# Layer 0's product of the attention with h by seven products on halves, in a two-layer graph kernel

## The chip, the cores and the metric

The kernel runs on one core of one Trainium2 chip. Its measure is the device time of one execution in microseconds, from start to end. An engine's name in the profile is short: PE is the tensor engine (PEld its loading of weights), DVE the vector engine, ACT the scalar engine, POOL the GpSimd engine, SP the queue that issues most transfers. All numbers are float32, and every result of PE goes to PSUM, which the program divides into banks of 512 float32 per partition.

## The reference

Sixteen graphs (B) of 1024 nodes (N) with 128 features (D) go through two layers. What matters here, with the names of the reference:

```python
h = jnp.einsum('bnf,df->bnd', x, Ww) + Wb                      # layer 0
e = jnp.einsum('bjl,bkl->bjk', jnp.einsum('bjd,dl->bjl', h, A), h)
e = e + jnp.swapaxes(e, 1, 2)
scores = jnp.where(adj > 0, e, 0.0)
attention = jax.nn.softmax(scores, axis=1) * adj
h_prime = jax.nn.relu(jnp.einsum('bij,bjk->bik', attention, h))
ic = jax.nn.sigmoid(h_prime @ wi_u + x @ wi_x)[..., None]      # fc, oc in the same way
x = _layernorm(x + oc * jnp.tanh(ic * h_prime + fc * x))

h = jnp.einsum('bnf,hfd->hbnd', x, conv_w) + conv_b            # layer 1, four heads
scores = jnp.einsum('hbni,hij,hbmj->hbnm', h, attn_w, h)
Ah = jnp.tanh(adj * scores)
hh = jax.nn.relu(jnp.einsum('hbnm,hbmd->hbnd', Ah, h))
x = _layernorm(x + jax.nn.relu(jax.nn.relu(jnp.mean(hh, axis=0)) + x))
```

The change concerns the one line `attention` times `h` of layer 0: a product of 1024 x 1024 by 1024 x 128 for each graph.

## The kernel before

**Passes and slots.** After a fill, the kernel makes 16 passes, one for each graph b (the loop at L1163). A pass has 32 steps: four heads of layer 1 by eight blocks of 128 rows. In each step PE makes two scores of layer 1 (`Pair.score`, L820, 512 columns each) and, between them, products of earlier steps (`early`, L905, and `late`, L913). Layer 1's product of tanh with h is already done by seven products on halves: `Pair.product` (L845) issues instructions of 64 output columns with 256 columns streamed, two side by side, and `differ` (L838), `differ_more` (L889) and `join_rows` (L788) make the sums and differences that it needs. `differ_more` does one addition on DVE and one by a DMA that accumulates, issued from POOL (L892). `mm` (L80) splits any other product into two instructions of 64 output columns with up to 512 streamed.

Each step has two *slots*, 64 in a pass. Everything else is a small piece with a name, and the lists `PLAN`, `FIRST` and `LAST` (L1128 to L1157), written out by hand, say in which slot each piece is issued. All engines take their work in the program's order, so the plan fixes every queue. A plain name is a piece of layer 0 of the next graph (b + 1), a name with `+` one of the graph after it (b + 2); `d`, `m`, `j`, `r` and `u` are pieces of layer 1, `e` the end of the last graph's layer 1.

**Layer 0 of one graph, by names.** `W`, `X`, `L` load x transposed, x and the rows of adj (the ring of three buffers, L372). `Q` and `H`, `h` make projections, among them h in `t["h"]` (L399). `S` (L419) makes the score blocks, of which only one triangle is computed, into the tile R of 8 x 8 blocks; `T` turns a block row through DRAM (`hop`, L292: one write, and four reads issued later by `land`). `E` makes a mask from adj on POOL (L475). `A` (L508) masks row j and takes its maximum (DVE, L492), negates that (L500, on DVE but for graph 0) and takes exponentials (ACT, L504). `B` (L512) multiplies row j by adj (DVE, L527) and scales h's row by the reciprocal sum (L524).

**The product in question.** `back(j)` (L531) adds row block j's share to the transposed result: for each half q of the 1024 nodes one `mm` with h's row block as weights and 512 columns of R streamed. For a graph b > 0 there is one PSUM bank, `acc0`, used in two turns: for half 0, `B` of each row calls `back` for the row before it; `R0` (L550) ends it and writes relu into `hpT`; then `G0` to `G7` make half 1 in the same bank, and `R1` ends it. In a middle pass `R0` stands in slot 18 (counted from 0), `G0` to `G7` and `R1` in 19 and 20.

**What follows it.** `P` (L610) turns `hpT` into rows (a transposition on DVE, L329, and a hop). `Y`, `F`, `f`, `i`, `o` make the gates from it: a product with the weights on POOL (L620), a sum on DVE (L626), a sigmoid. `I` (L659) and `O` (L671) make the layer's output, `Va` to `Vd` and `N` its layernorm, `D` turns it for layer 1.

**PSUM.** Three banks with the tag `sc` are shared by layer 1's scores and all projections and layer 0 scores, in turn; `acc1` to `acc3` hold layer 1's sums, `acc0` layer 0's.

## Time and profile before

| | us |
|---|---|
| median of 2 runs | 2328.44 (2328.14 to 2328.74) |
| the profiled execution | 2329.8 |
| its span, first to last instruction | 2328.0 |
| PE busy / PEld busy | 2304.9 / 1074.7 |
| DVE / ACT / POOL busy | 2039.5 / 1292.4 / 1308.2 |
| all DMA engines, share of the span: hardware queue, software queue | 38.8%, 18.1% |
| PE busy in the first 65 us / from 65 to 146 us | 62.76 / 77.09 |
| PE busy in the last 146 us | 138.44 |

One execution was profiled. Busy times say how long at least one instruction of an engine was under way; matmuls overlap, so a busy PE can be less than a full one. A group of the profile's list gives the line, the engine, the operation, what is written and read, the shape and the count, then busy time and mean duration in ns, and after a second bar the engine's idle time before such instructions and what ended it. One matmul instruction leaves two records in the trace[...]; two instructions of 64 columns that lie side by side run at once, so four records belong together. A pass takes 2328 / 16 = 145.5 us on average, the fill included.

### The profile page before, as it was taken

Reading aid. Unit: us, or ns where it says so; the run is one execution under the profiler, and the core shown is the slowest. Engines: PE = TensorE matmul, PEld = TensorE weight load, DVE = VectorE, ACT = ScalarE, POOL = GpSimd, SP = SyncE. Lnnn points to the kernel's source line nnn. Section 1 sums busy time; section 2 is a strip of 40 time slices with the busy share of each in tenths; the row PEclk is TensorE's granted clock in tenths of the full one; section 3 lists DMA queues with packets and bytes.
Section 4 is the critical chain, followed back from the end, with each engine's and each line's share of the span. In section 5 each row is a group of like instructions: output and inputs, shape, how many; then the busy total and the mean of one; then the engine's idle time right before and its main releaser. Section 6 shows DMA issues by size and latency. Waiting matters only on the chain. (4 is left out here: it accounts for less than half of the span.)

```text
span 2328.0 us, 40444 instructions
## 1 busy us (share of the span) xinstructions
PE 2304.9 (99%) x14693; PEld 1074.7 (46%) x14693; DVE 2039.5 (88%) x3689; ACT 1292.4 (56%) x2186; POOL 1308.2 (56%) x1129
## 2 busy tenths in 40 slices
PE   9999999999999999999999999999999999999998
PEld 5345544444444444444444444444444444444444
DVE  7879898998989889898898988889898898988777
ACT  6545564555556555555555555556556555554444
POOL 2645656556565655656466564665645646555342
PEclk9999999999999999999999999999999999999999
DMA  4647565575655656556565565756647565573421
GB/s 146 164 95 199 124 144 154 114 195 133 170 133 111 190 137 173 132 123 173 134 180 129 129 179 114 184 133 135 171 105 201 130 165 135 106 184 86 123 55 37
DMA packets 498090, 327.27 MB, mean 141 GB/s; under 512 B 391139, under 2 KB 416482, under 8 KB 497891
## 3 DMA queue, kind: packets, MB, share of 16 engines
q1 hardware_dynamic: 459149, 250.68, 38.8%
q0 software_dynamic: 38448, 73.94, 18.1%
q8 instruction: 116, 1.90, 0.3%
q14 instruction: 83, 0.68, 0.1%
q10 hardware_dynamic: 294, 0.07, 0.0%
HBM read 199.04 MB, written 59.51 MB: 111 GB/s over the span
## 5 line engine op out<-in xcount | busy, mean ns | idle before, releaser
L86 PE MATMUL sc<-uT,x1T 128*64 128x512 f32 x4096 | 1054.4, 593 | 4.0 <-ACT uT L283 1.9
L836 ACT ACTIVATE pair<-pair 128x1024 f32<-128x1024 f32 x504 | 533.3, 1058 | 588.9 <-DVE pair L829 278.7
L892 POOL DMA_DIRECT2D pair<-pair x252 | 225.5, 895 | 723.3 <-ACT pair L836 158.2
L831 DVE TENSOR_TENSOR pair<-sc,adj 128x512 f32<-128x512 f32 x504 | 339.1, 682 | 105.1 <-PE sc L86 103.7
L86 PEld LDWEIGHTS sc<-uT,x1T 128*64 128x64 f32 x4096 | 294.1, 137 | 293.8 <-issue 156.8
L829 DVE SCALAR_TENSOR_TENSOR pair<-sc,adj 128x512 f32<-128x512 f32 x504 | 343.0, 684 | 86.0 <-PE sc L86 81.5
L475 POOL TENSOR_SCALAR edge<-ring 128x1024 uint8<-128x1024 f32 x120 | 361.0, 3010 | 25.2 <-DMA ring<-in_adjT_dram 23.4
L840 DVE TENSOR_TENSOR pair<-pair 128x1024 f32<-128x1024 f32 x252 | 328.8, 1305 | 10.6 <-ACT pair L836 10.6
L864 PE MATMUL late<-pair,h 128*64 128x256 f32 x2016 | 304.8, 380 | 3.7 <-DMA pair<-pair 3.6
L864 PE MATMUL early<-pair,h 128*64 128x256 f32 x2016 | 304.1, 379 | 1.3 <-ACT pair L836 1.3
L864 PE MATMUL late<-pair,hx 128*64 128x256 f32 x2016 | 304.1, 380 | 0.0
L864 PEld LDWEIGHTS early<-pair,h 128*64 128x64 f32 x2016 | 145.3, 137 | 289.7 <-issue 255.2
L86 PE MATMUL acc<-R,h 128*64 128x512 f32 x960 | 232.2, 592 | 1.3 <-ACT h L524 1.3
L864 PEld LDWEIGHTS late<-pair,h 128*64 128x64 f32 x2016 | 145.6, 137 | 185.4 <-issue 129.5
L864 PEld LDWEIGHTS late<-pair,hx 128*64 128x64 f32 x2016 | 146.6, 137 | 178.3 <-issue 142.7
L891 DVE TENSOR_TENSOR pair<-pair 128x512 f32<-128x512 f32 x252 | 187.8, 745 | 3.2 <-PE early L864 2.6
L504 ACT ACTIVATE R<-R,nmax 128x1024 f32<-128x1024 f32 x126 | 144.7, 1148 | 62.8 <-DVE nmax L500 56.4
L492 DVE CUSTOM_DVE_ANT_0 R<-R,edge 128x1024 f32<-128x1024 f32 x120 | 172.8, 1440 | 3.3 <-POOL edge L475 3.0
L527 DVE TENSOR_TENSOR R<-R,ring 128x1024 f32<-128x1024 f32 x120 | 161.6, 1347 | 0.0
L864 PE MATMUL early<-pair,hx 128*64 128x256 f32 x1008 | 152.0, 379 | 0.0
L620 POOL TENSOR_TENSOR x1T<-hp,wu_b 128x1024 f32<-128x1024 f32 x45 | 111.7, 2482 | 69.5 <-DVE hws L626 63.3
L936 POOL TENSOR_TENSOR w<-w 128x512 f32<-128x512 f32 x63 | 84.8, 1346 | 96.5 <-DVE w L926 96.3
(214 smaller groups left out, 2831.2 us busy)
## 6 DMA issues: line engine op xcount, KB each, us to landing
adj<-in_adjT_dram SPq DMA_DIRECT2D x128, 512.0 KB, 4.2
pair<-pair POOLq DMA_DIRECT2D x252, 256.0 KB, 3.7
ring<-in_adjT_dram SPq DMA_DIRECT2D x120, 512.0 KB, 5.0
xT<-in_xT_dram SPq DMA_DIRECT2D x16, 512.0 KB, 7.2
x<-in_x_dram SPq DMA_DIRECT2D x16, 512.0 KB, 5.2
dram_hp<-turn_hp SPq DMA_DIRECT2D x15, 512.0 KB, 2.6
hp<-dram_hp SPq DMA_DIRECT2D x60, 128.0 KB, 3.1
dram_x<-turn_x SPq DMA_DIRECT2D x15, 512.0 KB
```

The lines of the kernel that those rows point to most:

```text
L86: nc.tensor.matmul(out[ts(c, HD)], lhsT[:, ts(c, HD)], rhs, start=start, stop=stop)
L475: engine.tensor_scalar(m, t["adj", j], 0.0, None, ALU.is_gt)
L492: nc.vector.tensor_tensor_reduce(to[:, ks], s[:, ks], t["edge", j][:, ks], 1.0, nmax, ALU.mult, ALU.max, top)
L504: nc.scalar.activation(row(j), row(j), AF.Exp, bias=t["nmax", j], accum_out=t["z", j])
L527: nc.vector.tensor_mul(s[:, ks], s[:, ks], adj[:, ks])
L829: nc.vector.scalar_tensor_tensor(to, psv, -1.0, adj, op0=ALU.mult, op1=ALU.mult)
L831: nc.vector.tensor_mul(to, psv, adj)
L836: nc.scalar.activation(s, s, AF.Tanh)
L840: nc.vector.tensor_add(t[:, X3 : N12 + 1 : N12 - X3, :], t[:, N12 : N12 + 1, :].to_broadcast([P, 2, 512]), t[:, B22 : B11 + 1, :],)
L864: nc.tensor.matmul(out[ts(q, HD)], w, self.t[:, at, ts(q, HN)], start=(i == 0 and p in (1, 3, 5, 4)), stop=(i == BH - 1), skip_group_check ...
L891: nc.vector.tensor_add(t[:, B22], t[:, B22], t[:, N12])
L892: nc.gpsimd.dma_start(t[:, N21], t[:, B22], accum_op=ALU.add)
```

## The change

For graphs from 1 on (graph 0, done in the fill, keeps its way), the product is made by seven products of halves in place of eight. R is cut into four quarters: `block(i, r)` is row block i or i + 4 and half 0 or 1 of the columns, r = 0 to 3. h is cut by row block (i or i + 4) and by feature half.

- `row_sides` (pieces `K0`, `K1`, `K2`) makes the sums and differences of h's quarters in place and in a new tile `x7`, nine subtractions on POOL.
- `product0` (pieces `a`, `c`, `p`, `q`, `y`, `x`, `z` with i = 0 to 3) issues two instructions of 64 by 256 each, 56 a pass.
- `add_blocks` (pieces `s`, `g`, `t`, `v`) adds quarters of R in place: for i = 3 on DVE, for i = 0 to 2 by an accumulating DMA issued from POOL. Between the products the order is: `c` reads quarter 3, `s` adds quarter 1 to 3, `p` reads 3, `g` adds 0 to 1, `q` reads 1, `t` adds 0 to 3, `x` reads 3, `v` adds 3 to 2, `z` reads 2.
- The bank `acc0` has three turns, begun by `a0`, `p0` and `y0`. `gather` (pieces `U1` to `U6`) brings each turn into `hpT`: U1 and U2 are copies on ACT, U3 to U6 additions and subtractions on DVE. `relu_rows` (`R1`) makes the relu there.
- The result's features stand in another order: Ww's transposed columns, Wb's row and the identity of the gate product are permuted when made, one small product is added to the weights' preparation (`p_gu`), and `P` uses `turn_sums` (eight reads with runs of 256 bytes) for `turn` (four with 128); `sum_hp` and `inner` index accordingly.
- The negation of the maximum (L500) moves to ACT for all graphs from 1 on, and `B` no longer calls `back` for them.
- The plans are written anew; pass 14 has one of its own, `NEXT`.

```diff
-            if b == 0 and j > 2:
+            if b or j > 2:
                 nc.scalar.mul(nmax, top, -1.0)
...
-            if j and (b or j not in (1, NB - 1)):
-                back(j - 1, [0] if b else range(NH))
+            if b == 0 and j not in (0, 1, NB - 1):
+                back(j - 1)
...
+        def block(i, r):
+            j, c = divmod(r, NH)
+            return t["R"][:, ts(c, BH), i + j * BH, :]
+
+        def row_sides(n):
+            if n == 0:
+                t["x7"] = sb.tile([P, BH, HD], F32, tag="x7", name=f"x7_{b}", bufs=1)
+            h = t["h"][:, :, :D].rearrange("p (m i) (e d) -> p m e i d", m=2, e=2)
+            g = (slice(0, 3), slice(3, BH), slice(0, BH))[n]
+            x = t["x7"][:, g]
+            a11, a21, a12 = h[:, 0, 0, g], h[:, 0, 1, g], h[:, 1, 0, g]
+            if n == 2:
+                nc.gpsimd.tensor_sub(x, x, a11)
+                return
+            nc.gpsimd.tensor_sub(a12, a11, a12)
+            nc.gpsimd.tensor_sub(x, a21, h[:, 1, 1, g])
+            nc.gpsimd.tensor_sub(a12, a12, x)
+            nc.gpsimd.tensor_sub(a21, a11, a21)
+
+        def product0(p, i):
+            if i == 0 and p in (2, 7, 1):
+                t["acc"] = ps_acc.tile([P, 512], F32, tag="acc0", name=f"acc0_{b}_{p}")
+            h = t["h"][:, :, :D].rearrange("p k (e d) -> p k e d", e=2)
+            j, e, r, at = {
+                2: (i + BH, 0, 2, 0), 3: (i + BH, 0, 3, 1), 7: (i, 1, 3, 0), 5: (None, 0, 1, 1),
+                1: (i, 0, 0, 0), 6: (None, 0, 3, 0), 4: (i + BH, 1, 2, 1),
+            }[p]
+            w = t["x7"][:, i] if j is None else h[:, j, e]
+            for q in range(NH):
+                nc.tensor.matmul(
+                    t["acc"][ts(q, HD), ts(at, HN)], w, block(i, r)[:, ts(q, 2)],
+                    start=(i == 0 and p in (2, 7, 1)), stop=(i == BH - 1),
+                    skip_group_check=True,
+                )
+
+        def add_blocks(n, i):
+            to, a = ((3, 1), (1, 0), (3, 0), (2, 3))[n]
+            to, a = block(i, to), block(i, a)
+            if i == BH - 1:
+                nc.vector.tensor_add(to, to, a)
+            else:
+                nc.gpsimd.dma_start(to, a, accum_op=ALU.add)
+
+        def gather(n):
...
+            if n == 1:
+                nc.scalar.copy(w[:, 0:2], acc)
+            elif n == 2:
+                nc.scalar.copy(w[:, 2:4], acc[:, 0:1].to_broadcast([P, 2, HN]))
+            elif n == 3:
+                nc.vector.tensor_sub(
+                    w[:, 1:4:2], w[:, 1:4:2], acc[:, 1:2].to_broadcast([P, 2, HN])
+                )
+            elif n == 4:
+                nc.vector.tensor_add(w[:, 0], w[:, 0], acc[:, 0])
+            elif n == 5:
+                nc.vector.tensor_add(
+                    w[:, 1:4], w[:, 1:4], acc[:, 0:1].to_broadcast([P, 3, HN])
+                )
+            else:
+                nc.vector.tensor_add(w[:, 2], w[:, 2], acc[:, 1])
+
+        def relu_rows():
+            w = t["hpT"].rearrange("p (k n) -> p k n", k=4)
+            nc.scalar.activation(w[:, 0:4:2], w[:, 0:4:2], AF.Relu)
+            nc.scalar.activation(w[:, 1:4:2], w[:, 1:4:2], AF.Relu, scale=-1.0)
...
-            turn(t["hp"], hpT, f"hp_{b}")
+            turn_sums(t["hp"], t["hpT"], f"hp_{b}")
...
+    PLAN = [
...
+        "r6 r3 m1 B5 L7", "", "E7 +L0 j0.1 e u1.0 A6", "a0 a1 +W", "B6 A7", "a2 u1.1 K0",
+        "d2 c0 c1 s0 +Q0 s1 m2 c2 B7 d3", "s2 a3 +Q1 K1", "e g0 g1 m3 g2 c3 U1 u2.0",
+        "s3 p0 e p1 j1.0", "e p2 q0 t0 e p3", "q1 g3 e U2 t1 t2", "q2 v0 q3 U3",
+        "y0 y1 t3 y2 v1 d4 y3 K2 U4 v2", "e x0 v3 x1 x2 m4 z0 x3", "z1 z2 z3 U5 U6 j1.1 R1",
+        "P d5 +H0", "m5 +h0", "j2.0 +E0", "+S0 e", "d6 m6", "u2.1", "+T0 Y j2.1", "e +L1 F",
...
+        "+S7 +B1 +L4", "+A2 +E3", "", "r4 u0.0 u0.1 d14 m14 r5 r0 d15 +A3 +B2 +T4 +T5 +L5 +B3 r1",
+    ]
...
-        plan = LAST if b + 1 == B else PLAN if b else FIRST
+        plan = FIRST if b == 0 else LAST if b + 1 == B else NEXT if b + 2 == B else PLAN
```

The parts of `PLAN` shown are slots 9 to 32 and the last four, 60 to 63. Between the pieces of two slots PE makes one score of layer 1 and one or two of its early or late products, so that a name in this list stands a known number of PE instructions behind any other.

## The prediction

> **What bounds the kernel now.** I read the page's totals first, then a table of stretches over middle passes, the tensor engine's timeline there, its waits, and last the groups of instructions and single lines.
>
> ```profile
> span 2328.0 us, 40444 instructions
> ...
> PE 2304.9 (99%) x14693; PEld 1074.7 (46%) x14693; DVE 2039.5 (88%) x3689; ACT 1292.4 (56%) x2186; POOL 1308.2 (56%) x1129
> ...
> PEclk9999999999999999999999999999999999999999
> ```
>
> PE is busy 99% of the span at full clock. A busy PE need not be a full one, so I look inside.
>
> ```profile
> core 0: us, PE busy (x) PEld busy (x) DVE busy (x) ACT busy (x) POOL busy (x), PEclk, DMA share, GB/s
> 582.00:728.00 146.00, 145.80 (x946) 66.66 (x942) 130.72 (x235) 82.18 (x140) 84.26 (x71) 1.00 0.61 147
> 1018.00:1164.00 146.00, 145.80 (x944) 66.63 (x942) 131.95 (x237) 82.26 (x138) 86.07 (x72) 1.00 0.60 146
> ```
>
> A middle pass has 0.2 us without PE work. DVE has about 15 us free in it (146 less 131), ACT 64, POOL 62.
>
> ```profile
> 681.46 5.32 PE L86 MATMUL acc<-R,h 128*64 128x512 f32 x24
> 686.61 1.03 PE L86 MATMUL sc<-uT,x1T 128*64 128x512 f32 x4
> 687.47 0.60 PE L864 MATMUL early<-pair,h 128*64 128x256 f32 x4
> 687.90 1.89 PE L86 MATMUL acc<-R,h 128*64 128x512 f32 x8
> 689.61 1.03 PE L86 MATMUL sc<-uT,x1T 128*64 128x512 f32 x4
> ```
>
> The columns are start, duration and count; durations overlap, so the price is the distance between starts. Four records (two instructions of 64 columns, side by side) of 512 cost 687.47 - 686.61 = 0.86 us; 24 of them 5.15, six times 0.86. Four records of 256 cost 687.90 - 687.47 = 0.43, exactly half: the narrower form loses nothing.
>
> ```profile
> PE late L864 <- DMA pair<-pair: 3.6, 4, 1.2
> PE sc L86 <- DVE h L411: 3.1, 12, 0.8
> ...
> PE acc L86 <- ACT h L524: 1.3, 1, 1.3
> ```
>
> The worst of PE's waits are a few us in the whole run. So the kernel is bound by the number of matrix columns streamed, and every us of stream removed is a us of time, if nothing comes late.
>
> **The change, part by part.**
>
> *Stream removed.* The groups give the count:
>
> ```profile
> L86 PE MATMUL acc<-R,h 128*64 128x512 f32 x960 | 232.2, 592 | 1.3 <-ACT h L524 1.3
> ...
> L892 POOL DMA_DIRECT2D pair<-pair x252 | 225.5, 895 | 723.3 <-ACT pair L836 158.2
> ```
>
> 960 records are 240 groups of four, 16 in each of 15 passes: 240 x 0.86 = 206.4 us. After, a pass has 7 products x 4 row blocks x 2 instructions of 256 = 28 groups at 0.43; 15 x 28 x 0.43 = 180.6. PE's stream falls by 25.8 us, 1.72 a pass. One more 128x3 product in the weights' preparation costs at most 0.3 (the row of a 128x128 product is 278 ns), once.
>
> *DVE, per pass.* Added: four block additions (i = 3) at 0.745 (the 128x512 addition of L891) = 3.0; the gathers 3 to 6: one like L926 (128x512 from PSUM, 0.687), two of 256 columns like L925 (0.42), and one of 768, not in the trace: between 0.687 and two of these, 1.37; by the step from 256 to 512 it is 0.95, taken. Together 2.5. Removed: eight negations at 0.154 = 1.2. Net +4.3, so 131 becomes some 135 in a pass of 143.6. DVE's 15 us of free time hide it; they shrink to about 8.5. Without that cover the 4.3 us would be paid, more than twice the gain.
>
> *ACT.* Two copies of 0.58 (L900's first form) for U1 and U2, eight negations at some 0.2 (L632's 128x16 takes 0.217); the two ReLUs only change shape (0.6 each, L548). +2.8 on 82, hidden by 60 us of idle. Below nothing is possible too: with the negation on ACT an exponential no longer crosses from DVE for it; I take nothing.
>
> *POOL.* Twelve accumulating DMAs to issue at 0.895 = 10.7 and nine subtractions: four of 128x192, four of 128x64, one of 128x256. L797 takes 0.457 for 128 columns and L936 1.275 for 512, about 2.1 ns a column: 4 x 0.59 + 4 x 0.32 + 0.73 = 4.4. Together +15 on 85, of 143.6: 70% busy. The sum has cover; the order matters (below).
>
> *DMA and SP.* L892's transfers are 66 of the software queue's 74 MB, and that queue fills 18.1% of 16 engines' span: 2328 x 0.181 x 66/74 / 252 = 1.5 us of all engines each. Twelve add 18 us a pass to a share of 0.61 (89 us). The hp rows are read back by eight DMAs with runs of 256 bytes, no longer four with 128, so 2048 packets fewer; at the hardware queue's mean (38.8% x 2328 x 16 / 459149 = 31 ns) that gives back 4 us. SP issues four more at 0.68; its queue has about 1100 issues in the run, a third of the span. Hidden. The loads of x, xT and the ring change slots; SP takes its issues in order, so a load that waits for its buffer holds back the hops behind it. That costs nothing while what a hop brings is used slots later (a slot is 145.5 / 64 = 2.3 us on average), and at most the hop's own 2.5 to 3.1 us of landing where it is used at once; taken nothing, as the new plan leaves slots between them.
>
> *Waits added on PE, all in front of layer 1's scores, since PE takes its work in order.* Read off the new order, in PE's own us:
> 1. c0 needs the first three subtractions of K0, which may only start after a2. Between them lie a projection, a score and a late product: 2.58 us. The subtractions take 3 x 0.59 = 1.8, and more when POOL is held up: L796 has a median of 773 ns against L797's 457. Nothing to 1.5; taken 0.1.
> 2. a3 needs row block 7 weighted (L527, mean 1.35) by DVE, which stands behind a score eviction, a 1.3 and a 0.745 addition and a reciprocal. From the score that releases this to a3 PE has 4.3 us of other work; the DVE row sums to 0.68 + 1.3 + 0.75 + 0.16 + 1.35 = 4.2. No slack: nothing to 1.4; taken 0.2.
> 3. One PSUM bank in three turns: p0 waits for U1's copy on ACT, with 2.58 us of PE work in between, while ACT has a 0.58 and a 0.37 copy, a 1.06 tanh and then U1's 0.58 to do. Nothing to 2.6; taken 0.2. y0 waits for U3 on DVE, with 1.7 us for a 0.69 operation behind one eviction; 0.1.
> 4. The pass boundary. Slot 63 now issues rows 2 and 3 of the next layer 0 at once: on DVE a mask (1.44), two weightings, two small turns, two pair additions; on ACT the first tanh of the next pass stands behind the exponentials of row 4 (1.15 and 0.19) and two copies. Adding rows from the end of the pass's last score: exponentials 3 end at 7.3 us (behind the evictions of two projections and r0), the weighting of row 3 at 8.6, an eviction and the mask of row 4 at 10.4, exponentials 4 at 11.9, the copies at 12.9, the tanh at 13.9; PE, with nothing late, wants it at 13.3. Nothing to 0.9; taken 0.3.
> 5. Block additions: see the second rival. Taken nothing.
>
> That is 0.9 a pass, 13.5 us in 15.
>
> *A rule against the change.* L840 adds two operands from SBUF:
>
> ```profile
> L840 DVE TENSOR_TENSOR pair<-pair x252: 1198/1217/2607, 72.6 to 2289.5; 128x1024 f32<-128x1024 f32 x126
> ...
> L797 POOL TENSOR_TENSOR hx<-hx,h x126: 453/457/1411, 62.2 to 2260.4; 128x128 f32<-128x128 f32 x126
> ```
>
> Its mean of 1305 is 107 above its least, with single ones at twice the length. The Trainium skill ("SBUF — State Buffer", section "Who interferes with whom") says that DVE with two SBUF inputs and GpSimd exclude each other on a shared port pair, one waiting for the whole instruction of the other. By the rows, some 45 such DVE operations a pass lose 0.1 each, 4.5 us; POOL's arithmetic grows from 70 to 75 us, so 7% more: 0.3 us. By the rule at its worst all nine new POOL operations (4.4 us) stand in DVE's way, and the four new additions wait half of a 2.9 us mask (L475): +10, DVE over 143 of 143.6 and no slack left. The means hold such collisions already; I take 0.3, within DVE's free time.
>
> **Sum.** The profiled execution took 2329.8 (span 2328.0 and 1.8 around it), 1.4 above the median. 2329.8 - 25.8 + 13.5 = 2317.5; less 1.4: about 2316.
>
> **Rivals.**
> *The gain is eaten by small waits* (2326 to 2340). DVE's margin falls from 15 to 8.5 us; points 1 to 4 come to a third of their upper bounds together: (1.5 + 1.4 + 2.6 + 0.9) / 3 = 2.1 a pass, 1.2 above what I took, 18 us: about 2334. For it: these points have hardly any slack. Against it: the old order was also 90% full on DVE and lost 0.2 us a pass. 20%.
>
> *Slower: the chain of accumulating DMAs becomes late.* Rows t, v and product z hang together: t0 is issued after p0, v0 may be issued only when t0 has landed and holds POOL's queue until then (with K2 behind it, on which x0 waits, and the pair additions of layer 1), and z0 waits for v0 to land. In PE's time z0 comes 14.2 us after p0; before t0 POOL does four subtractions (j1.0, 2.8 us after it is free). With the page's 3.7 from issue to landing v0 lands some 10.2 us after p0: 4 us to spare. Fifteen transfers of 1.5 us (three are layer 1's) fall into some 27 us, 83% of the DMA engines. Every us of extra landing counts twice; beyond 5.7 PE waits, beyond 6.6 the 1.72 are lost. At twice the landing (7.4): 3.4 us a pass, 51 in all, in place of some of the 13.5 and not all on top: about 2358. For it: stretches with a DMA share of 0.97 exist. Against it: the big loads stand mostly outside these slots. 14%, a third of it over 2376.
>
> *The change does not do what it says*: the stream is read off the new order (56 instructions of 256 in place of 32 of 512 a pass), so only the time of a 256 in this layout (two pieces of 128 with a stride) could differ; the old form read four such pieces at full rate. With 10% lost, 18 us: 2334, counted with the first rival.
>
> *Better*: points 1 to 4 cost next to nothing, as in the old plan, which was as full, and PE's idle time outside the middle passes (23 us in the run, all but some 3 of it in the first and last two passes) falls by a few us with the new plans: 2300. 6%.
>
> **Numbers.** Forecast 2303 to 2326: 60%; the others as above. Range 2301 to 2340: it leaves out the slow rival and part of the last case. 2% (about what a measurement of this kernel can tell from no change) is 46.6 us: faster than 2282 would need nearly twice the removed stream, 2% out of the last case; slower than 2375: 5%; within: 93%.
>
> **What would show it.** PE busy near 2280; the new product lines with 1680 records and starts 0.43 apart; middle passes of about 144 us with under 1 us of PE idle; DVE near 2100; 180 new DMA issues on POOL. The forecast is wrong if PE shows waits of over 1.7 us a pass for K0, for the weighted row 7, for U1 or U3, for the tanh behind exponentials 4, or for a block addition's DMA; each names its step.

## The result, and the profile after

| | us |
|---|---|
| kernel before, median | 2328.44 |
| changed kernel, median of 2 runs | 2458.59 (2455.93 to 2461.25) |
| ratio, 95% interval | 1.056 (1.051 to 1.061) |
| forecast (range) | 2316 (2301 to 2340) |

The change makes the kernel 130 us slower. With the stream that it saves (25.8 us) it should have come to about 2303, so 156 us are to be explained. These are the page's totals after, in the lines that answer to those shown of before, and those of the software queue (packets, MB, share of 16 engines):

```profile
span 2459.5 us, 42745 instructions
...
PE 2326.8 (95%) x15415; PEld 1153.8 (47%) x15415; DVE 2078.0 (84%) x3690; ACT 1320.5 (54%) x2336; POOL 1534.2 (62%) x1444
...
PEclk9899999999999999999999999999999999999999
...
q0 software_dynamic: 133488, 121.14, 35.1%
```

PE idles 2459.5 - 2326.8 = 132.7 us, where it idled 23.1 before: 110 us are plain waiting. Its busy time should have fallen to 2279 and rose to 2327; the granted clock (mean 0.994, before 0.998; the one 8 in its row) is 9 us of those 48. An estimate of some 20 more: neighbouring products overlap in the record (four records of 256 last 0.60 us and start 0.43 apart), so a wait costs about 0.17 us beyond the idle time that it shows, and there are 151 waits where there were 31. The last 19 or so were not taken apart. No other engine comes near its limit: DVE went from 88 to 84% of the span. Now a stretch over a middle pass:

```profile
core 0: us, PE busy (x) PEld busy (x) DVE busy (x) ACT busy (x) POOL busy (x), PEclk, DMA share, GB/s
560.00:710.00 150.00, 143.17 (x970) 70.08 (x968) 130.24 (x230) 82.00 (x147) 97.99 (x93) 1.00 0.77 161
```

A pass had 0.2 us without PE work and has about 7. By the starts of the turn of the sums (once in a pass), 13 middle passes take 150.5 us each, before 142.7; 141.0 were due. The 9.5 us lost in each are 133 in 14 passes; most of the rest lies before the second pass' turn, which comes at 257.2 and came at 240.7. The tensor engine's waits in the whole run (total, times, longest):

```profile
PE early L951 <- ACT pair L923: 33.9, 39, 1.6
PE acc L586 <- POOL h L572: 15.6, 12, 2.0
PE late L951 <- DMA pair<-pair: 15.6, 18, 2.6
PE acc L586 <- DMA R<-R: 14.5, 20, 1.1
PE sc L86 <- ACT R L442: 9.0, 13, 0.7
```

Five more groups have 3 to 9 us each, L568 5.7 and L537 4.3 among them. Of 125 us of waits in all, 43 stand in front of the new products (L586) and 82 in front of everything else; before, all waits together were 16. No wait is long; there are nine or ten in each pass. One pass, from the tensor engine's timeline (a bracket gives the idle time before and what ended it):

```profile
687.06 1.08 PE L86 MATMUL sc<-uT,x1T 128*64 128x512 f32 x4 [0.31 <-ACT h L873]
692.44 0.65 PE L951 MATMUL early<-pair,h 128*64 128x256 f32 x4 [0.86 <-ACT pair L923]
695.58 0.65 PE L951 MATMUL early<-pair,h 128*64 128x256 f32 x4 [1.62 <-ACT pair L923]
727.15 0.83 PE L586 MATMUL acc<-R,h 128*64 128x256 f32 x4 [1.24 <-POOL h L572]
738.37 1.08 PE L586 MATMUL acc<-R,x 128*64 128x256 f32 x8 [0.48 <-DMA R<-R]
745.01 1.51 PE L586 MATMUL acc<-R,x 128*64 128x256 f32 x12 [0.39 <-POOL x L568]
750.06 1.08 PE L586 MATMUL acc<-R,h 128*64 128x256 f32 x8 [0.95 <-DMA R<-R]
783.51 1.08 PE L86 MATMUL sc<-xT,qT 128*64 128x512 f32 x4 [0.69 <-ACT R L442]
809.65 0.65 PE L951 MATMUL early<-pair,h 128*64 128x256 f32 x4 [0.40 <-ACT pair L923]
812.56 0.65 PE L951 MATMUL late<-pair,h 128*64 128x256 f32 x4 [0.32 <-DMA pair<-pair]
```

The four in the middle (3.06 us) stand in front of the new products: c3 waits for K1's subtractions, the others for a block addition's DMA or for K2. The six outside (4.20 us) do not touch the new products at all: they are a score of layer 1 behind a projection's copy (0.31) and layer 1's tanh (2.48) at the pass boundary, a score block of the next layer 0 (0.69), and two waits later in the pass, which I call the tail (0.72). That split gives the two theories: *the order* (the plan was rewritten everywhere, and is tighter than the old one) and *the block additions* (their DMAs and GpSimd's queue).

The boundary, in the same execution's timeline of all engines:

```profile
681.38 2.66 DVE L502 CUSTOM_DVE_ANT_0 R<-R,edge 128x1024 f32<-128x1024 f32 x1
681.59 3.10 POOL L485 TENSOR_SCALAR edge<-ring 128x1024 uint8<-128x1024 f32 x1
...
688.83 1.03 PE L86 MATMUL sc<-uT,x1T 128*64 128x512 f32 x4
...
691.04 2.79 DVE L537 TENSOR_TENSOR R<-R,ring 128x1024 f32<-128x1024 f32 x1
...
691.39 3.10 POOL L485 TENSOR_SCALAR edge<-ring 128x1024 uint8<-128x1024 f32 x1
...
693.75 0.68 DVE L916 SCALAR_TENSOR_TENSOR pair<-sc,adj 128x512 f32<-128x512 f32 x1
...
694.47 1.06 ACT L923 ACTIVATE pair<-pair 128x1024 f32<-128x1024 f32 x1 [1.79 <-DVE pair L916]
```

The score that PE starts at 688.83 is ready at 689.7, 0.86 us later, and DVE evicts it at 693.75, four us late. DVE is behind: slot 63 gave it mask A3, weightings B2 and B3 and turns T4 and T5 together, and slots 0 and 2 add A4 and B4. Two of these operations, A3 (681.38) and B4 (691.04), last 2.7 us where the median of their lines is 1.2, each while GpSimd begins a mask of its own (L485). The tanh at 694.47 had waited 1.79 us for DVE, and PE's product waits for that tanh.

### The profile page after: what moved, and what is told of

It reads as the page before. It is cut to its first block, busy times and chain, and to the rows that moved or that the text cites. A ratio compares the mean times of both kernels' runs of the same rounds, so it can differ in the third digit from the quotient of the medians.

```text
span 2459.5 us, 42745 instructions
## 1 busy us (share of the span) xinstructions
PE 2326.8 (95%) x15415; PEld 1153.8 (47%) x15415; DVE 2078.0 (84%) x3690; ACT 1320.5 (54%) x2336; POOL 1534.2 (62%) x1444
## 3 DMA queue, kind: packets, MB, share of 16 engines
q0 software_dynamic: 133488, 121.14, 35.1%
## 4 chain that ended last, share of the span: by engine, by line
PE 39%; DVE 19%; DMA 15%; POOL 9%; issue 4%; ACT 2%; SPq 2%; DVEq 0%; POOLq 0%; ACTq 0%
PE sc L86 19%; PE late L951 8%; DMA R<-R 7%; PE early L951 6%; DMA pair<-pair 4%; DVE pair L927 3%; DVE pair L916 3%; POOL R L599 2%; DVE pair L918 2%; DVE R L502 2%; SPq L328 2%; PE acc L586 2%; DVE R L537 2%; PE pR L86 2%; PE pT_u L86 2%
## 5 line engine op out<-in xcount | busy, mean ns | idle before, releaser
L86 PE MATMUL sc<-uT,x1T 128*64 128x512 f32 x4096 | 1072.9, 597 | 13.2 <-DVE pair L916 8.1
L923 ACT ACTIVATE pair<-pair 128x1024 f32<-128x1024 f32 x504 | 532.0, 1056 | 633.4 <-DVE pair L916 413.0
L979 POOL DMA_DIRECT2D pair<-pair x252 | 258.9, 1027 | 646.9 <-PE sc L86 126.6
L916 DVE SCALAR_TENSOR_TENSOR pair<-sc,adj 128x512 f32<-128x512 f32 x504 | 341.9, 683 | 125.7 <-PE sc L86 123.6
L918 DVE TENSOR_TENSOR pair<-sc,adj 128x512 f32<-128x512 f32 x504 | 339.6, 679 | 116.3 <-PE sc L86 115.7
L86 PEld LDWEIGHTS sc<-uT,x1T 128*64 128x64 f32 x4096 | 303.5, 137 | 255.5 <-issue 82.9
L485 POOL TENSOR_SCALAR edge<-ring 128x1024 uint8<-128x1024 f32 x120 | 378.3, 3153 | 9.4 <-DMA ring<-in_adjT_dram 8.2
L951 PE MATMUL early<-pair,h 128*64 128x256 f32 x2016 | 311.7, 382 | 34.1 <-ACT pair L923 33.9
L951 PE MATMUL late<-pair,h 128*64 128x256 f32 x2016 | 312.3, 382 | 15.7 <-DMA pair<-pair 15.6
L951 PE MATMUL late<-pair,hx 128*64 128x256 f32 x2016 | 311.6, 381 | 0.0
L951 PEld LDWEIGHTS early<-pair,h 128*64 128x64 f32 x2016 | 148.8, 137 | 329.9 <-issue 216.6
L599 POOL DMA_DIRECT2D R<-R x180 | 260.1, 1707 | 57.9 <-DMA R<-R 38.0
L951 PEld LDWEIGHTS late<-pair,h 128*64 128x64 f32 x2016 | 152.5, 138 | 197.2 <-issue 109.4
L951 PEld LDWEIGHTS late<-pair,hx 128*64 128x64 f32 x2016 | 154.8, 138 | 174.4 <-issue 135.6
L586 PE MATMUL acc<-R,h 128*64 128x256 f32 x1200 | 174.7, 383 | 32.5 <-POOL h L572 15.6
L537 DVE TENSOR_TENSOR R<-R,ring 128x1024 f32<-128x1024 f32 x120 | 171.6, 1430 | 0.0
L502 DVE CUSTOM_DVE_ANT_0 R<-R,edge 128x1024 f32<-128x1024 f32 x120 | 167.0, 1392 | 2.0 <-DMA R<-dram_turn 0.9
L951 PE MATMUL early<-pair,hx 128*64 128x256 f32 x1008 | 155.0, 381 | 2.0 <-POOL hx L885 1.8
L86 PE MATMUL sc<-xT,qT 128*64 128x512 f32 (+3 forms) x684 | 130.2, 486 | 13.2 <-ACT R L442 9.0
```

The costliest lines, as they stand in the source:

```text
L86: nc.tensor.matmul(out[ts(c, HD)], lhsT[:, ts(c, HD)], rhs, start=start, stop=stop)
L485: engine.tensor_scalar(m, t["adj", j], 0.0, None, ALU.is_gt)
L502: nc.vector.tensor_tensor_reduce(to[:, ks], s[:, ks], t["edge", j][:, ks], 1.0, nmax, ALU.mult, ALU.max, top)
L537: nc.vector.tensor_mul(s[:, ks], s[:, ks], adj[:, ks])
L586: nc.tensor.matmul(t["acc"][ts(q, HD), ts(at, HN)], w, block(i, r)[:, ts(q, 2)], start=(i == 0 and p in (2, 7, 1)), stop=(i == BH - 1), sk ...
L599: nc.gpsimd.dma_start(to, a, accum_op=ALU.add)
```

## The experiments

Times are medians, ratios are to the kernel before on the same chip (2329 to 2331). In line names the labels of the changed kernel are used; where an edit adds lines they shift by a few.

### Taking the change apart

**b_plan: the new order with the old product.** The pieces of the seven products are replaced by the old ones (row blocks 0 to 7 of half 0 at a0 to c3, of half 1 at p0 to q3); the names s, g, t, v, x, y, z and K do nothing. The negation of the maximum is on ACT, as in the changed kernel.

```diff
 (before, with the changed kernel's PLAN, FIRST, NEXT, LAST)
-            if b == 0 and j > 2:
+            if b or j > 2:
                 nc.scalar.mul(nmax, top, -1.0)
...
+            for j, name in enumerate(("a0", "a1", "a2", "c0", "c1", "c2", "a3", "c3")):
+                pieces[name] = partial(back, j, [0])
+            for j, name in enumerate(("p0", "p1", "p2", "q0", "p3", "q1", "q2", "q3")):
+                pieces[name] = partial(back, j, [1])
```

> The kernel before, with the old product (eight products, no block additions) issued from the new plan: a, c and p, q carry the old row products of 0.86 us, K, s, g, t, v, y, x, z do nothing, and the negation is on ACT. Theory 1 (the block additions and what they do to POOL and the DMA engines make the loss): about 2330 to 2345 us, as before. Theory 2 (the new plan crowds rows 2 and 3 into the last slot, and PE waits behind tanh at each pass boundary whatever the product): 2328 plus the after-profile's waits for tanh (34 us), for layer 0's evictions (9), for score evictions (13), and their tails: 2385 to 2400.

Measured 2455.0, ratio 1.054 (1.052 to 1.055). Its waits:

```profile
PE late L866 <- DMA pair<-pair: 48.6, 30, 3.8
PE early L866 <- ACT pair L838: 31.8, 39, 1.6
PE sc L86 <- ACT R L432: 9.0, 13, 0.7
```

With none of the new products, additions or DMAs the kernel is as slow as the changed one. The waits of L432 (L442 after) are the changed kernel's, those of early nearly (31.8 for 33.9), with the same single waits of 0.85 and 1.62 at the pass boundary. One part is of the experiment's own making: slots 22 to 24 lose the work of y, x and z, and late waits about 2 us in each pass there for the pair's DMA, some 31 us. Less that, the order costs about 2424 - 2331 = 93 us. This is an estimate: no run shows that these 31 us would come back in full, the old product puts twice the new one's stream into the slots of a, c, p and q, and the negation's move to ACT is counted in.

**c_noadd: without block additions.** Neither DVE nor DMA adds blocks; the products read blocks that were not added.

```diff
     def add_blocks(n, i):
+        return
```

> The changed kernel with all block additions of R left out (neither DMA nor DVE adds them, so part of the product is missing). Theory 1: the waits for K1, K2, the block DMAs and layer 1's pair DMAs vanish (52 us and tails), about 2390 us. Theory 2: the boundary waits stay, the others are a small part: 2415 to 2440 us.

Measured 2411.4, ratio 1.034 (1.032 to 1.036): 47 us less than the changed kernel.

```profile
PE early L952 <- ACT pair L924: 30.9, 38, 1.6
PE late L952 <- DMA pair<-pair: 27.6, 23, 2.7
PE sc L86 <- ACT R L442: 9.0, 13, 0.7
```

All waits in front of the new products for K1, K2 and the DMAs are gone, those of the order have stayed, and late's for the pair's DMA has grown from 15.6 to 27.6. Both theories hold, the order with the larger part: without any additions the kernel is still 108 us above the 2303 that were due (the nine subtractions and the gathers are in that).

**c2_nodveadd: the DMAs alone.** Only the four additions on DVE are left out.

```diff
             if i == BH - 1:
-                nc.vector.tensor_add(to, to, a)
+                return
```

> The changed kernel without the four block additions that the vector engine makes in a pass (those of row block 3 are left out; the twelve accumulating DMAs stay). With neither kind it took 2411. Theory 'the DMAs and their issue are the price of the block additions': 2445 to 2460. Theory 'the vector engine is too full': 2410 to 2425, nearly all that leaving both out gave.

Measured 2457.7, ratio 1.055 (1.052 to 1.057). DVE is busy 47 us less and the time stays. So DVE's four additions are not the price; what c_noadd gave back comes with the twelve DMAs of a pass.

**e_pooladd: the twelve DMAs as GpSimd additions.**

```diff
-            nc.gpsimd.dma_start(to, a, accum_op=ALU.add)
+            nc.gpsimd.tensor_add(to, to, a)
```

> The changed kernel with the twelve block additions of a pass done by POOL's own additions (1.28 us each by the row of a 128x512 addition on POOL) in place of accumulating DMAs (1.71 us to issue, 5.7 to land). Theory 1: the landing and the descriptor work go, but POOL's additions compete with DVE: 2400 to 2430 us. Theory 2: the boundary is untouched, 2440 to 2460 us.

Measured 2488.5, ratio 1.068 (1.064 to 1.071). An addition takes 1.6 us of GpSimd, about the 1.7 that a DMA's issue took in the mean, and DVE, whose busy time rises from 2078 to 2197, is now late with the row weighting (L537: 30.1 us of waits) and its own additions (21.4).

**f_oldplan: the seven products in the old order.** The new pieces are put at slots 13 to 26 of the old plan, where the old product had ended.

```diff
-    "B7 j1.1 j1.0", "d3", "+L0 m3 e X R0 e", "+E0 G0 G1 G2 e e e G3 G4 G5",
+    "B7 j1.1 j1.0 c0 c1 s0 s1 c2", "d3 s2 a3 K1", "+L0 m3 e X e g0 g1 g2 c3 U1", "+E0 e e e s3 p0 p1",
```

> The changed kernel's product in the old plan: every piece but the product's stretch (slots 13 to 26) and the gates after it stands where it stood before. Theory 1: the additions' costs stay, 2390 to 2430 us. Theory 2: the boundary waits go, and with them 60 us and more: 2370 to 2395 us.

Measured 2740.6, ratio 1.177 (1.174 to 1.180), with 114.3 us of waits for L572 and the clock at 0.968. The products need an order of their own; this one was not tuned and says nothing of the best that keeps the old frame.

### The boundary

**h_crowd: the kernel before with only its boundary changed.** Rows 2 to 5 of the next layer 0 are given to slot 63 and to slots 0 to 3, as in the new order.

```diff
-    "+A2 u0.1 +A3", "+L4", "d14 r5 r0 m14 r4 +B2 d15 r1",
+    "+A2 u0.1", "+L4", "r4 d14 m14 r5 r0 d15 +A3 +B2 +T4 +T5 +L5 +B3 r1",
```

> The kernel before, its old product of 512 columns kept, with one thing moved: at the pass boundary rows 2 to 5 of the next pass are issued in slot 63 behind the last rows, as the changed kernel does. Theory 'crowded boundary': the waits of early on the pair appear here as well, without any product on halves: 2350 to 2370. If the boundary is harmless by itself: 2325 to 2335.

Measured 2432.8, ratio 1.045 (1.043 to 1.046).

```profile
PE acc L86 <- ACT h L524: 51.2, 14, 3.8
PE late L864 <- DMA pair<-pair: 26.4, 25, 2.7
```

The crowded boundary costs 103 us in the old kernel, more than expected, and by another wait: the old product's pieces stand right behind each row's weighting, so PE waits for the weighted row (L524), 3.66 us a time, and the tanh is hardly late (1.5 us in the run). So the changed kernel's wait is neither confirmed nor refuted here: PE stands still for the weighted row, and the tanh has that time.

**d_boundary: the changed kernel with the old boundary.**

```diff
-    "+S7 +B1 +L4", "+A2 +E3", "", "r4 u0.0 u0.1 d14 m14 r5 r0 d15 +A3 +B2 +T4 +T5 +L5 +B3 r1",
+    "+L4 u0.0", "+A2 u0.1 +A3", "", "d14 r5 r0 m14 r4 +B2 d15 r1",   # slots 0 to 10 and 53 to 59 to match
```

> The changed kernel with slots 53 to 63 and 0 to 10 put back to the spread of the old plan: the last pair of row blocks, its projections and its evictions go back into the next pass, so that layer 0's last rows and the tanh of the next pass no longer follow at once. Everything else, the seven products too, stays. Theory 'crowded boundary': the two waits of early and the one of late on the pair (L923) at the start of a pass, with the slowed clock behind each, go away, 35 to 45 us: about 2410 to 2425, the wait group of L923 below 15 us. Theory 'the seven products and their DMAs': 2445 or more, and the waits only change places.

Measured 2537.3, ratio 1.090 (1.088 to 1.092): the wait went, and the time rose by 79 us. Its waits, and then GpSimd's timeline at the boundary:

```profile
PE late L951 <- DMA pair<-pair: 59.9, 24, 4.4
PE early L951 <- POOL hx L885: 19.9, 15, 1.4
...
PE early L951 <- ACT pair L923: 8.9, 18, 1.4
```

```profile
700.32 2.76 POOL L485 TENSOR_SCALAR edge<-ring 128x1024 uint8<-128x1024 f32 x1 [3.08 <-DMA ring<-in_adjT_dram]
703.04 0.90 POOL L979 DMA_DIRECT2D pair<-pair  x1
```

The wait for L923 fell from 33.9 to 8.9, as the theory said. But the load of row 4 now comes later, GpSimd's mask waits 3.08 us for it, and behind the mask, in GpSimd's queue, stands the pair's accumulating DMA, which PE needs next: late waits 3.6 us at this place.

**d_mix** spreads the second half of the pass like the old order as well.

```diff
-    "I0 +S4 I1", "d9", "m9 O0", "+T2 +L2",
+    "+S3 +T2", "d9 I0", "m9 I1", "+S4 O0 +L2",
```

> The changed kernel with the order of the old plan everywhere but in slots 11 to 32, where the seven products stand. Theory 'crowded plan' (boundary and the second half of the pass too): 2385 to 2405, with waits left only for L572, the accumulating DMAs and L568, some 35 us together. Theory 'the products and their DMAs': 2440 or more, since their waits are all inside the slots that are kept.

Measured 2692.0, ratio 1.157 (1.155 to 1.158): late for the pair's DMA 61.3, scores for ACT's copies 49.8, early for the tanh 43.1. **d3_turns** takes only T4, T5 and B3 out of slot 63.

```diff
-    slot 63: "... d15 +A3 +B2 +T4 +T5 +L5 +B3 r1"   slot 0: "E4 L6 A4"   slot 1: "j0.0 m15 E5"
+    slot 63: "... d15 +A3 +B2 +L5 r1"               slot 0: "E4 A4"      slot 1: "j0.0 m15 B3 L6 E5"
+    slot 58: "+T4"   slot 62: "+T5"
```

> The changed kernel with three pieces taken out of slot 63: the turns T4 and T5 go to slots 58 and 62, row 3's weighting B3 to slot 1 of the next pass. Nothing else moves. Theory 'the vector engine has too much to do at once at the boundary': the wait of early for L923 falls from 34 to below 18 us, 2420 to 2440. If PE lacks other work there, or the waits only change places: 2450 to 2470.

Measured 2523.5, ratio 1.082 (1.079 to 1.086): the tanh still costs 32.6, late rises to 36.8, L918 to 22.9. **d2_boundary** was to mend d_boundary by issuing m15 ahead of the mask.

```diff
+    slot 0: "m15"   slot 1: "j0.0 E4 B3 L6"   slot 60: "+B1 +L4"   slot 62: "u0.1 +A3"
```

> A second try of the spread boundary of d_boundary, now with the pair's DMA (m15) and the join of h (j0.0) issued ahead of row 4's mask, which there waited for its row of the adjacency and held them up 3.6 us. Theory 'too much at once at the boundary': the waits for L923, for the pair's DMA and for L885 together below 40 us (65 in the changed kernel's boundary and tail, 89 in d_boundary), 2400 to 2435. If the waits are a fixed sum that changes places: 2450 or more.

Measured 2587.1, ratio 1.110 (1.108 to 1.112). m15 now stands ahead of a product that read the value it overwrites, so that product reads another operand and waits 8 us a pass for the DMA (106.4 in all). It says nothing of the boundary.

**x_cover: other work for PE at the boundary.**

```diff
-    slot 4: "d0"         slot 11: "E7 +L0 j0.1 e u1.0 A6"
+    slot 4: "d0 u1.0"    slot 11: "E7 +L0 j0.1 e A6"
```

> The changed kernel with one projection of PE (u1.0, 0.86 us) moved from slot 11 to slot 4, just ahead of the second waiting product at the boundary. Theory 'no other work for PE there': the wait for L923 falls by about 0.86 in each of 14 passes, 12 us, and the time by 10 to 20 us with the clock behind it: 2440 to 2450. If slot 11 needed it as cover just as much: within 6 us of the changed kernel, with a new wait near slot 11 or 14.

Measured 2460.6, ratio 1.056 (1.054 to 1.057).

```profile
PE early L951 <- ACT pair L923: 19.0, 30, 1.4
...
PE sc L86 <- DVE pair L916: 16.0, 17, 4.4
...
PE early L951 <- POOL hx L885: 9.1, 13, 1.2
```

The wait for the tanh fell by 14.9 us; 7.1 came back at the same boundary, where PE now waits for DVE's eviction (L916), and 7.3 at L885, in front of the place from which the projection was taken. That is the second case of the expectation: the same sum at other places.

**n_split: GpSimd's mask in four pieces.**

```diff
-            engine.tensor_scalar(m, t["adj", j], 0.0, None, ALU.is_gt)
+            for part in (ts(c, N // 4) for c in range(4)) if b else [slice(N)]:
+                engine.tensor_scalar(m[:, part], t["adj", j][:, part], 0.0, None, ALU.is_gt)
```

> The changed kernel, GpSimd's mask of a row of the adjacency (L485, 128x1024, about 3 us) made in four pieces of 256 columns. Nothing is moved and nothing left out. Theory 'two-operand work of the vector engine waits for the whole GpSimd operation beside it' as the cause of the late tanh at the pass boundary: the operations of 2.7 us on L502 and L537 become at most 2 us, the wait of early for L923 falls from 34 to below 15 us, and the time to 2415 to 2440. If the boundary is late by its order alone: wait and time as in the changed kernel, 2450 to 2465.

Measured 2528.4, ratio 1.084 (1.082 to 1.087). These are the groups of the mask on GpSimd and of the masking on DVE:

```profile
L486 POOL TENSOR_SCALAR edge<-ring 128x256 uint8<-128x256 f32 x480 | 549.9, 1283 | 7.4 <-DMA ring<-in_adjT_dram 7.3
...
L503 DVE CUSTOM_DVE_ANT_0 R<-R,edge 128x1024 f32<-128x1024 f32 x120 | 155.7, 1298 | 10.8 <-POOL edge L486 6.8 <-DMA R<-dram_turn 0.7
```

And these are weighting B4 and the second product that waits for a tanh at a pass boundary (L538 and L952 are L537 and L951 here):

```profile
707.47 1.29 DVE L538 TENSOR_TENSOR R<-R,ring 128x1024 f32<-128x1024 f32 x1
...
710.50 0.65 PE L952 MATMUL early<-pair,h 128*64 128x256 f32 x4 [0.24 <-ACT pair L924]
```

The masking's mean falls from 1392 to 1298 ns and the wait for L923 from 33.9 to 21.1. At the boundary B4 takes 1.29 us for 2.79, and the second wait falls from 1.62 to 0.24 in this pass and to at most 0.25 at every boundary; the first stays at 0.64 to 0.96. So the second wait is the work of the collision with the mask. But a mask in four pieces keeps GpSimd busy for 549.9 / 120 = 4.6 us where one piece took 3.15, and early now waits 41.9 us for GpSimd's hx. **v_both** adds u_merge's edit (below) to it.

> Both of the last two edits in the changed kernel: the mask in four pieces and the merged DMAs. If each works by itself and the gains add up: 2385 to 2420. If a wait that is removed comes back at the next stage, as it did with K1's subtractions on the vector engine: 2440 or more. The kernel before (2329) is out of reach either way.

Measured 2522.4, ratio 1.084 (1.079 to 1.088): no gain over n_split.

### The block additions

**k1_dve: K1's four subtractions on DVE.**

```diff
-            nc.gpsimd.tensor_sub(a12, a11, a12)
+            engine = nc.vector if n else nc.gpsimd
+            engine.tensor_sub(a12, a11, a12)   # and the other three
```

> The changed kernel with the four subtractions of K1 (row block 3, 64 columns each) on the vector engine, so that they no longer stand behind accumulating DMAs on the GpSimd queue. Theory 'issuing these DMAs holds GpSimd': the wait of acc for L572 (15.6 us in 12, and the slowed clock behind it) goes, 2435 to 2447. Theory 'the subtractions were late for their inputs': the wait stays, now on the vector engine, 2455 to 2465.

Measured 2468.6, ratio 1.060 (1.058 to 1.062). The wait for L572 is gone (15.6 to nothing), that for R's DMAs grew from 14.5 to 25.0 and that for the pair's from 15.6 to 28.5. **w_k1** issues K1 on GpSimd ahead of the DMA s2.

```diff
-        "s2 a3 +Q1 K1",
+        "a3 K1 s2 +Q1",
```

> The changed kernel with K1's four subtractions issued on GpSimd before the accumulating DMA s2 and not behind it. Theory 'K1 is late because it stands behind that DMA': the wait for L572 falls from 15.6 to below 5 us and the time by 12 to 20 us, unless s2 itself then lands late for p2 (acc for R<-R DMA, 14.5 us now, would grow). If the fixed sum holds: within 6 us of the changed kernel's time.

Measured 2465.4, ratio 1.060 (1.057 to 1.063). GpSimd's timeline at K1, first of the changed kernel, then of w_k1:

```profile
722.37 2.72 POOL L599 DMA_DIRECT2D R<-R  x1
723.50 1.95 POOL L570 TENSOR_TENSOR h<-h 128x64 f32<-128x64 f32 x1
723.78 1.94 POOL L571 TENSOR_TENSOR x<-h 128x64 f32<-128x64 f32 x1
```

```profile
728.04 0.48 POOL L570 TENSOR_TENSOR h<-h 128x64 f32<-128x64 f32 x1
728.37 0.43 POOL L571 TENSOR_TENSOR x<-h 128x64 f32<-128x64 f32 x1
728.88 0.32 POOL L572 TENSOR_TENSOR h<-h,x 128x64 f32<-128x64 f32 x1
...
729.67 3.92 POOL L599 DMA_DIRECT2D R<-R  x3 [0.20 <-issue]
```

In this pass a subtraction of 64 columns lasts 1.95 us behind s2 and under 0.5 ahead of it (over the run L570's mean falls from 1.89 to 0.74), and the wait for L572 is gone: the theory of K1's delay is right. But s2 now lands late in K1's place, and the wait for R's DMAs goes from 14.5 to 32.9. **u_merge** makes one DMA of two neighbouring row blocks, 8 for 12 in a pass.

```diff
+            first, last = ((0, 1), (0, 1), (1, 2), (1, 2))[n]
+            if i == first:
+                return
...
+            to, a = (
+                t["R"][:, ts(r % NH, BH), r // NH * BH + (first if i == last else i) :
+                       r // NH * BH + i + 1, :]
+                for r in (to, a)
+            )
+            nc.gpsimd.dma_start(to, a, accum_op=ALU.add)
```

> The changed kernel with the accumulating DMAs of two neighbouring row blocks made one: 8 for 12 in a pass, the same bytes, but runs of 256 elements in place of 128 for half of them or more. Theory 'number of runs': issue stays near 1.7 us for each, so GpSimd issues 7 us a pass less, the waits for L572 and L568 (21 us) fall to below 10, and the time to 2425 to 2445. Theory 'bytes': a merged DMA takes 2.5 us or more to issue, the waits stay, 2450 to 2470.

Measured 2455.1, ratio 1.053 (1.050 to 1.056), an interval that overlaps the changed kernel's. The issue takes 1.47 us each in the mean, 168 us in all for 260; the waits for L572 fall to 5.1, and those for R's DMAs rise to 29.7: a merged DMA is issued in the place of its second part, and lands 6.3 us after its issue where a single one took 5.7. Neither expectation fits whole.

**y_dve2 and z_dveall: additions on DVE.** Leaving out DVE's additions had given nothing, so DVE seemed to have room.

```diff
-            if i == BH - 1:
+            if i >= BH - 2:          # z_dveall: i >= 0
                 nc.vector.tensor_add(to, to, a)
```

> The changed kernel with the block additions of row block 2 on the vector engine too (eight there, eight by accumulating DMA; it was four and twelve). Theory 'the price is GpSimd's queue': the waits for L572, L568 and the DMA of R (36 us) fall below 15, 2420 to 2440. Theory 'they cost the same anywhere' (the vector engine then passes its 3 us a pass on): 2450 to 2475.

> All sixteen block additions of a pass on the vector engine, no accumulating DMA of R left. Its load grows by 9 us a pass, to some 140 of 150. Theory 'the price is GpSimd's queue' alone: between 2411 (the additions left out) and 2435. Theory 'the vector engine is then the bound': the waits on L537 and L916/L918 take the place of those on GpSimd and the DMAs, 2460 to 2520.

y_dve2: 2418.8, ratio 1.038 (1.036 to 1.040), 40 us less than the changed kernel and within 8 of c_noadd, which adds no blocks at all. z_dveall: 2453.2, ratio 1.053 (1.051 to 1.055). The waits of y_dve2:

```profile
PE early L951 <- ACT pair L923: 36.1, 41, 1.6
PE late L951 <- DMA pair<-pair: 25.6, 33, 2.7
...
PE sc L86 <- ACT R L442: 9.0, 13, 0.7
```

The waits for K1, K2 and R's DMAs, 36 us together, are gone at once, against 10 us more for the pair's. Two things changed together and were not separated: GpSimd issues four DMAs fewer (the others land in 4.5 us for 5.7), and row block 2, the last of each group that went by DMA, no longer waits for a landing. All sixteen additions on DVE are too many: hpT (L612) 18.8 and L537 15.8 us of waits. Of the versions tried with the seven products and all additions, y_dve2 is the fastest; it remains 90 us above the kernel before, though it streams 26 less. Its largest waits are those of the order; K's subtractions and the gathers have a part that was not measured by itself.

## Why the prediction was wrong, point by point

The step that failed is the sum of PE's waits: 0.9 us a pass, 13.5 in all. A middle pass lost 9.5. Its terms were too small for the pass boundary (wait 4) and for the block additions (wait 5), and the rest of the rewritten order had no term.

*Stream removed, 25.8 us.* Right: the new products have 1200 + 480 records, 28 groups of four in each of 15 passes, and where nothing waits they start 0.43 us apart.

*DVE, +4.3 a pass, hidden.* (2078.0 - 2039.5) / 15 = 2.6, and hidden: four additions less change nothing, and y_dve2 with four more is faster. DVE's total was not the bound. That it is behind by four us for a short stretch, at the boundary, a total cannot show.

*POOL, +15 a pass.* (1534.2 - 1308.2) / 15 = 15.1: right in sum, which is luck, since busy spans overlap and the parts are wrong. The issue was taken at 0.895, the row of the pair's DMA. R's take 1.707 in the mean, and 1.28 where one stands alone:

```profile
L599 POOL DMA_DIRECT2D R<-R x180 | 260.1, 1707 | 57.9 <-DMA R<-R 38.0
```

```profile
740.57 1.28 POOL L599 DMA_DIRECT2D R<-R  x1 [2.18 <-DMA R<-R]
```

I took a row with the same bytes and overlooked another layout: the pair's DMA moves runs of 2 KB, R's a quarter of a row block, four runs of 512 bytes in a partition.

*DMA, 1.5 us of all engines each.* (2459.5 x 0.351 - 2328.0 x 0.181) / 180 = 2.46, for the same reason; the landing took 5.7 us, and 3.7 was used.

*Waits 1, 2 and 3* (K0, row 7, U1 and U3; taken 0.1, 0.2, 0.3). About right: K0 is in time, row 7 (L537) costs 4.3 us in the run, hpT 1 to 2. K1, in front of c3, I did not price at all: 15.6 us, the largest wait of the new products.

*Wait 4, the pass boundary* (taken 0.3, bounded by 0.9). In the pass shown it is 2.48, in two waits. The first, 0.86, is the one that I summed: the sum itself gave 13.9 - 13.3 = 0.6, of which I took half, and mask A3, put in with its mean of 1.44, took 2.66. The second, 1.62, stands at ten of the run's pass boundaries and had no term at all: the chain ended at the first tanh, and B4, behind it on DVE, took 2.79 us and held back the eviction for the next tanh. With B4 at 1.29 (n_split) 0.24 is left of it. The port rule that I weighed (the Trainium skill, "SBUF — State Buffer", "Who interferes with whom") was rightly worth little in DVE's total; I did not ask where its single collisions of some 1.5 us would fall. The trace follows the rule only in part: neither operation waited for a whole mask of 3.1 us, and sixteen of L502's that began inside a mask took 1.18 to 1.25.

*Wait 5, block additions* (taken nothing; the second rival, 2358). In the pass shown the waits for R's DMAs and for K2 behind them are 1.8 us, with K1 3.06; left out, the additions give back 47 us. That the rival's size (51 us, at a landing of 7.4) is so near is luck: the landing took 5.7, at which by its own sum PE does not wait yet. In the run 14.5 us are waits for landings and 21.3 are for subtractions (K1, K2) in GpSimd's queue, which the rival named for K2 alone.

*What was never asked.* "The new plan leaves slots between them" and "the old plan was as full" stood in for an examination of the rest of the order. The prediction priced waits at pieces that are new and took every old piece as still in time, although the diff rewrites all 64 slots. L442 (0.69) and the tail (0.72) are such pieces. The old order lost 0.2 us a pass; that spoke for the old order, and I carried it over to the new one. b_plan shows what that was worth: the order with the old product costs some 93 us. With the block additions' 47 and the stream's -26 that makes 2328 + 93 + 47 - 26 = 2442 of 2459.

*Still open.* That DVE is behind at the boundary is seen in the trace, and n_split shows what makes the second wait there. That easing the boundary alone would give the time back was not shown: each of five edits moved the sum to another queue or another slot, or made it larger. Why the new order as a whole waits more than the old one is known only wait by wait. Whether there is an order for the seven products as tight as the old one was for the old product was not settled either.

## What to carry to other kernels

When a change rewrites an order, take nothing over from the old one: price every piece of the critical engine against its producers in the new order, and test the order alone with the old work. An engine with 15% of idle time can still be four us behind where several of its pieces are issued together, so ask for its backlog at the place, and follow the chain past the first piece that it delays. Cost a DMA from a row with the same runs and not merely the same bytes, and count the instructions that stand behind its issue.

## What the runs showed of the hardware

- An accumulating DMA issued from GpSimd costs the issuing engine by its number of runs, not by its bytes. Where the issue stands alone (medians), the pair's 256 KB take 0.90 us, R's 256 KB 1.28, and u_merge's 512 KB in as many runs as R's 1.30. The software queue's packets count the runs: (38448 / 267 DMAs) 144 for each before, (133488 - 38448) / 180 = 528 for each of R's. The Trainium skill ("DMA: Bandwidth & Descriptors", "Anatomy of one DMA — SWDGE (gpsimd) path") says that many descriptors can be emitted before an incremental cost shows; here 384 more packets take 0.38 us of the queue.
- GpSimd's arithmetic right behind such issues is recorded up to six times as long: 128x64 subtractions of 1.95 us, where they take 0.31 to 0.36 without these DMAs (c_noadd). The two spans overlap each other and the DMA's (722.37 to 725.09), so they hold waiting as well as work.
- A GpSimd operation over 1024 columns took 3.15 us; in four pieces of 1.28 in the mean, whose spans overlap, it keeps the engine busy for 4.6.
- PE's clock pays for the longer waits once more. In the changed kernel, from 150 us on, the granted clock was 0.50 for 3.4 us right after each of the four waits of 1.96, 2.12, 2.25 and 2.64 us (from 1030.4, 1283.0, 2221.6 and 2303.5), and after none of the shorter ones, up to 1.63. At half clock 3.4 us do the work of 1.7.
